# Cross-attention stack: pieces ordered by a model of four engine queues, and other group sizes

## The chip, the cores and the metric

The kernel runs on one core of one Trainium2 chip. The metric is the device time of one execution in microseconds (us), lower is better. The profile below was taken by the hardware profiler from one execution. Its engines are PE (TensorE matmuls), PEld (TensorE weight loads), DVE (VectorE), ACT (ScalarE), POOL (GpSimd) and SP (which issues most transfers). "L1326" is line 1326 of the kernel. The granted clock is the share of TensorE's full clock that the chip let it have.

## What is computed

Four transformer blocks follow one another on x of 4 x 1024 tokens, 288 wide; a context of 64 tokens per batch element is attended to in each. There are 16 heads of 18. Blocks 0 and 3 are alike and are the ones that matter here:

```python
h = layer_norm(x, ln1_g, ln1_b, 1e-06); q8, s, sm = quant_act(h)
... # self-attention with quantised q, k, v and output products
h = layer_norm(x, ln2_g, ln2_b, 1e-05)
q8, s, sm = quant_act(h)
q = quant_linear(q8, s, sm, wq2, bq2)
k = cond @ wk2.T + bk2; v = cond @ wv2.T + bv2
a = attn(q, k, v, mask)
a8, sa, sma = quant_act(a)
x = x + quant_linear(a8, sa, sma, wo2, bo2)
h = layer_norm(x, ln3_g, ln3_b, 1e-05)
q8, s, sm = quant_act(h)
h = gelu(quant_linear(q8, s, sm, wfc1, bfc1))     # 288 -> 1152
q8, s, sm = quant_act(h)
return x + quant_linear(q8, s, sm, wfc2, bfc2)    # 1152 -> 288
```

`quant_act` finds each token's largest magnitude, divides by it and rounds to levels -127 to 127. Block 1 attends without normalisation to the context in two parts (ordinary and "prompt" keys, each with a softmax and weights of its own) and adds both outputs to x. Block 2 is a block with tensor-wide quantisation; it is not touched.

## The kernel before

x stays in SBUF as 32 tiles of 128 tokens. Everything runs in one program, in order: block 0's self-attention (`quant_self`), then a stage of block 0's context attention and feed-forward with block 1's attention woven in, then block 2 (`fq_attn`), then block 3's self-attention, then block 3's context attention and feed-forward. Block 0 and block 3 share the code in `quant_net`; the argument `vip` tells them apart (it holds block 1's weights, and is given with block 0 only).

The stages in question are made of generators, one per group of tokens. A generator issues some instructions and yields; each stretch between two yields is a piece. `run_stages` holds the active generators and chooses which one goes on next, so the choice sets the order in which pieces are written down. It keeps one clock, `now`. A piece says how much PE time it takes, which moves `now` on, and how long after that its next piece may follow, a constant wait such as 6.0. A third value names the ACT table that the next piece needs: `EXP` or `GELU`. A piece of the other table than the last is put off until nothing else is ready or until it has waited 6 us. Among the ready ones the earlier stage in the list goes first. A layer underneath then places the instructions of each engine, by the order of writing and by what is ready, and inserts the waits.

The generators are:

- `ctx_stage`, context attention, 8 groups of 512 tokens (two to a batch element). A group takes its statistics (`norm_stats_of`, DVE), is normalised (`norm_apply`: ACT at L1377, then POOL times gain and plus bias, L1380 and L1381), rounded by `levels` (DVE maximum L1302, scale L1304, reciprocal L1306, then per tile DVE L1310 and ACT L1311; PE transposes L1326, ACT copy L1331), and its token scales are spread over columns (`scale_cols` DVE L2283, PE L2293, ACT L2298). A loop over four head groups follows, skewed by one step per operation: query product L2152, DVE L2160, scores L2168, ACT exponential L2171, values L2179, ACT copy L2187, transposes L2195, DVE L2198 to L2208. The result goes through `levels` again, and `level_residual` multiplies (L277), scales (DVE L1722) and adds to x (POOL L1723). The keys and values of a batch element are fetched by its first group (L2121, L2122) at the very start of that group.
- `ff_stage`, feed-forward, 16 groups of 256 tokens: statistics per 512 tokens, normalisation, output bias added to x (`add_bias`, POOL L1727), `levels` with six extra columns (`three_parts`, POOL L1587 and L1589), first product L277 with scaling and maximum on DVE (L2246), GELU on ACT (L2264, and L2266 for the maximum), `levels` again, second product, and the residual. In block 3 the tokens are then stored.
- `vip_aside`, once, in block 0: forms block 1's keys and values on PE (L2472, L2509) and stores them.
- `vip_tokens`, block 1, 16 groups of 256 tokens: transposes L2379 and L2384, query product L2399 and L2403, copies L2535, scores L2556, exponential L2564, sums L2575, reciprocal L2583, spread L2588, scaling L2597, output L2606, and the sum into x L2616.

In block 0 one context group, two feed-forward groups and two block-1 groups are active at once; in block 3 two context groups and three feed-forward groups. A feed-forward group may begin when its context group is done, a block-1 group when its feed-forward group is done. In block 0 the context and feed-forward pieces use four PSUM banks and block 1's another four; block 3 uses all eight.

Of the kernel before, what the change touches and what calls it, by code (L numbers as in the profile page):

```python
# [28 lines left out]
F32 = mybir.dt.float32  # L29
# [13 lines left out]
NG = 4  # L43
# [8 lines left out]
EXP, GELU = "exp", "gelu"  # L52
# [1126 lines left out]
class Fast(Net):  # L1179
# [60 lines left out]
    def run_stages(self, stages):  # L1240
# [5 lines left out]

        state = [{"next": 0, "busy": 0, "done": set()} for _ in stages]
        active, mode, now = [], None, 0.0

        def begin():  # L1250
            for st, sg in zip(state, stages):
                while (
# [5 lines left out]
                    active.append({"st": st, "sg": sg, "n": n, "at": now, "kind": None})  # L1258
# [5 lines left out]
        while active:  # L1264
            ready = [a for a in active if a["at"] <= now]
            if not ready:
                now = min(a["at"] for a in active)
                continue
            late = [a for a in ready if a["kind"] not in (None, mode)]
            same = [a for a in ready if a["kind"] in (None, mode)]  # L1270
            if late and (not same or now - min(a["at"] for a in late) > 6.0):
                a = min(late, key=lambda a: a["at"])
                mode = a["kind"]
            else:
                a = same[0]
# [3 lines left out]
            said = next(a["sg"][0][a["n"]], None)  # L1279
            self.pb, self.wk = outer  # L1280
            if said is None:
# [3 lines left out]
            else:  # L1285
                now += said[0]
                a["at"] = now + said[1]
                a["kind"] = said[2] if len(said) > 2 else None
# [3 lines left out]
    def levels(self, h, am, width, tag, terms=0, bufs=2):  # L1292
# [6 lines left out]
        kc = (n + terms) // width  # L1299
        if am is None:  # L1300
# [13 lines left out]
        yield 0, 6.0 if kc == n // P else 5.0  # L1314
# [3 lines left out]
        per, most = (2, kc) if kc == NC3 else (1, 5)  # L1318
        for j0 in range(0, m, per):
# [17 lines left out]
            yield 0.07 * per * kc, 1.5 if j0 + per == m else 0  # L1337
# [669 lines left out]
    def quant_net(self, L, w, ctxT, mask, out, ready=None, vip=None):  # L2007
# [4 lines left out]
        with ExitStack() as es:  # L2012
# [30 lines left out]
            for k, v in (("sw", cw["swo"]), ("b", w["bo2"])):  # L2043
                cw["wo"][k] = fp.tile([P, C], F32, name=f"wo2{k}")
                nc.sync.dma_start(cw["wo"][k], v.partition_broadcast(P))
            nb = 1 if vip else 2
            cp = pool(f"{L}cb", nb)
# [6 lines left out]
            rext = fp.tile([P, 2, 2 * B * NG], F32, name="rext")  # L2054
# [3 lines left out]
            ff_gens = self.ff_stage(g3, b3, w1, w2, tops, out, nb + 1)  # L2058
            stages = [
                (ctx_gens, nb, lambda i, d: True, None),  # L2060
                (ff_gens, nb + 1, lambda i, d: i // 2 in d[0], None),
            ]
            if vip:
# [13 lines left out]
                parts = self.key_parts(vp)  # L2077
                prep, vk = ExitStack(), []
                pk = prep.enter_context(tc.tile_pool(name="vn", bufs=1))

                def vip_pools():
                    if not vk:
# [11 lines left out]
                        lambda i, d: i in d[1] and 0 in d[2],  # L2094
# [7 lines left out]
            for n, (t, what) in enumerate(  # L2102
                ((rext, "wt"),) + (((ext, "vwx"),) if vip else ())
            ):
# [5 lines left out]
    def ctx_stage(self, cw, g2, b2, pool, nb):  # L2110
# [5 lines left out]
        keys = {}  # L2116
# [8 lines left out]
        def tokens(b, hf):  # L2125
            t0 = b * NTB + hf * 4
            if hf == 0:
                fetch(b)
            kbd, vbd = keys[b]
            stats = self.norm_stats_of(t0, 4, 1e-5)  # L2130
            yield 0, 7.0
            h = self.wk.tile([P, 4, C], F32, tag="h", name="h", bufs=nb)
            for j in range(4):
                self.norm_apply(h[:, j, :], t0 + j, stats, g2, b2, t0)
                if j % 2:
                    yield 0, 1.0 if j == 1 else 9.0
            hT, sc = yield from self.levels(h, None, CK, "x", 0, nb)
            srep = self.wk.tile([P, 512], F32, tag="srep", name="srep", bufs=nb)
            for j in (0, 2):
                two = sc[:, j : j + 2]  # L2140
                cols = self.scale_cols(two)
                yield 0, 1.0
                self.over_tokens(two, srep[:, j * P : (j + 2) * P], cols)
            yield 0.8, 1.0
            a = self.wk.tile([P, 4, C], F32, tag="h", name="a", bufs=nb)
            qs, es_, os_ = {}, {}, {}
            for n in range(NG + 3):
                g = n
                if g < NG:
# [11 lines left out]
                    yield 0.65, 0 if n else 1.0, EXP if n else None  # L2161
                g = n - 1
                if 0 <= g < NG:
# [10 lines left out]
                    yield 0.9, 0 if n > 1 else 1.0  # L2174
                g = n - 2
                if 0 <= g < NG:
# [11 lines left out]
                    yield 0.9, 0.5  # L2188
# [1174 lines left out]
```

## Time and profile before

| | us |
|---|---|
| median of 3 runs | 5224.39 (5214.77 to 5228.77) |
| the profiled execution, its own time | 5225.67 |
| its span, first to last instruction | 5224.0 |
| PE busy in the span | 4411.4 (84%) |
| ACT busy | 3066.3 (59%) |
| DVE busy | 2965.4 (57%) |
| POOL busy | 1316.5 (25%) |
| block 0's context and feed-forward with block 1 | 895 to 1707 |
| block 3's context and feed-forward | 4737 to the end |

Busy means that an instruction of that engine was running. Matmuls are pipelined, so a busy PE is not PE at its peak. Over the whole kernel PE is the busiest engine, but that share is an average over stages; the two stages that the change touches have other shares, which are read by windows. A wait in the list of waits is idle time of one engine just before an instruction, put down to what came last of that which it waited for. The mean granted clock of the whole span is 0.833.

### The profile page before, as it was taken

To read this page: it belongs to the slowest core of one execution; us is meant where nothing else is said; L and a number is where in the kernel's file an instruction comes from. 1 tells how busy PE (TensorE), PEld (TensorE's weight loads), DVE (VectorE), ACT (ScalarE), POOL (GpSimd) and SP (SyncE) were. 2 spreads that over 40 slices of the span, in tenths; PEclk is the share of its full clock that TensorE was granted. 3 is DMA by queue.
4 is the path that set the end of the run, shared out by engine and by line. 5 is a ranking of instruction groups with operands and counts; after the bars stand their busy time and mean duration, and the time that the engine had idled before them with its cause. 6 is when DMAs were issued, how large, how long until landed. Compare 5 with 4: busy or idle time off the path is not lost. (4 is left out here: it accounts for less than half of the span.)

```text
span 5224.0 us, 63236 instructions
## 1 busy us (share of the span) xinstructions
PE 4411.4 (84%) x23067; PEld 1784.7 (34%) x23067; DVE 2965.4 (57%) x6518; ACT 3066.3 (59%) x4313; POOL 1316.5 (25%) x1949
## 2 busy tenths in 40 slices
PE   5999997788888879999688873899998999996676
PEld 2223222455555431100133331454542223222334
DVE  7333244555555559999788777432334333344776
ACT  2767665455454239999788863212215766664676
POOL 4010111232322457400122225111104021003553
PEclk9999998889899975555688785899997999997778
DMA  2000002200000221000000022000000000001000
GB/s 74 4 5 12 3 21 61 80 3 14 16 12 23 90 91 38 21 0 0 21 24 25 21 96 79 24 14 10 1 10 6 8 4 9 18 21 39 12 12 20
DMA packets 135538, 135.62 MB, mean 26 GB/s; under 512 B 69260, under 2 KB 111884, under 8 KB 133552
## 3 DMA queue, kind: packets, MB, share of 16 engines
q1 hardware_dynamic: 134016, 127.79, 8.1%
q0 software_dynamic: 1200, 3.69, 0.3%
q8 instruction: 183, 3.00, 0.2%
q14 instruction: 139, 1.14, 0.1%
HBM read 79.59 MB, written 43.47 MB: 24 GB/s over the span
## 5 line engine op out<-in xcount | busy, mean ns | idle before, releaser
L1980 ACT ACTIVATE e<-ps 128x1024 f32<-128x1024 f32 x1024 | 998.9, 1021 | 484.3 <-PE ps L1970 473.5
L1970 PE MATMUL ps<-qT,kT 32*128 32x512 f32 x4096 | 705.3, 661 | 8.2 <-ACT e L1980 8.2
L1930 PE MATMUL ps<-e,v 128*32 128x512 f32 x4096 | 571.1, 623 | 10.4 <-DVE oT L1941 9.1
L2853 DVE TENSOR_REDUCE top<-e 128x2 f32<-128x2048 f32 x256 | 561.9, 2275 | 18.6 <-ACT e L2846 18.6
L2846 ACT ACTIVATE e<-ps 128x1024 f32<-128x1024 f32 x512 | 534.1, 1369 | 19.6 <-PE ps L3199 11.3
L3248 ACT ACTIVATE e<-ps 128x1024 f32<-128x1024 f32 x512 | 484.4, 1056 | 92.2 <-PE ps L3239 74.6
L3199 PE MATMUL ps<-qk 32*128 32x512 bf16 x1024 | 510.9, 604 | 24.5 <-ACT e L2846 23.2
L1723 POOL TENSOR_TENSOR x<-x,y 128x288 f32<-128x288 f32 x192 | 151.0, 798 | 980.7 <-DVE y L1722 966.1
L1380 POOL TENSOR_TENSOR h<-h,g 128x288 f32<-128x288 f32 x224 | 181.0, 810 | 721.8 <-ACT h L1377 702.6
L3251 DVE TENSOR_SCALAR eb<-e 128x2048 bf16<-128x2048 f32 x256 | 322.1, 1261 | 50.0 <-ACT e L3248 47.8
L1970 PEld LDWEIGHTS ps<-qT,kT 32*128 32x128 f32 x4096 | 205.5, 189 | 230.3 <-issue 143.1
L2846 ACT ACTIVATION_READ_ACCUMULATOR e<-ps 128x1 f32 x512 | 280.9, 550 | 0.0
L3239 PE MATMUL ps<-qk,kz 64*128 64x512 bf16 x1024 | 231.1, 449 | 41.8 <-ACT e L3248 39.2
L2399 PE MATMUL psf<-hT,w 128*128 128x512 f32 x576 | 257.9, 600 | 0.6 <-ACT hT L2391 0.6
L1377 ACT ACTIVATE h<-x,nmr,rstd 128x288 f32<-128x288 f32 x224 | 129.4, 622 | 185.8 <-DVE nmr L1369 102.5
L1326 PE MATMUL ps<-idb,q 128*128 128x128 bf16 (+2 forms) x1152 | 108.5, 245 | 151.0 <-ACT q L1311 106.8
L1930 PEld LDWEIGHTS ps<-e,v 128*32 128x32 f32 x4096 | 83.0, 109 | 421.3 <-issue 348.0
L3199 PEld LDWEIGHTS <-qk 32*128 32x128 bf16 x1024 | 52.8, 99 | 465.1 <-issue 465.1
L3148 ACT ACTIVATE gl<-psf,bf 128x512 f32<-128x512 f32 x72 | 46.0, 684 | 270.4 <-PE psf L2403 265.8
L277 PEld LDWEIGHTS <-qT 98*128 98x128 bf16 (+2 forms) x1344 | 138.7, 107 | 134.8 <-issue 51.5
L1381 POOL TENSOR_TENSOR h<-h,b 128x288 f32<-128x288 f32 x224 | 178.7, 800 | 0.3
L3152 DVE SCALAR_TENSOR_TENSOR u<-psf,bf,gl 128x512 f32<-128x512 f32 x72 | 51.2, 747 | 213.3 <-ACT gl L3148 213.0
(480 smaller groups left out, 7706.9 us busy)
## 6 DMA issues: line engine op xcount, KB each, us to landing
raw<-y SPq DMA_DIRECT2D x32, 432.0 KB
in<-raw SPq DMA_DIRECT2D x32, 432.0 KB
kz<-qk SPq DMA_DIRECT2D x128, 64.0 KB
wn<-in_L_wfc SPq DMA_DIRECT2D x12, 432.0 KB
x<-in_x SPq DMA_DIRECT2D x4, 1152.0 KB
vvo<-vt SPq DMA_DIRECT2D x16, 288.0 KB
vo<-vvo SPq DMA_DIRECT2D x4, 1152.0 KB
rawq<-y SPq DMA_DIRECT2D x32, 144.0 KB
```

The lines of the kernel that those rows point to most:

```text
L1380: nc.gpsimd.tensor_tensor(h, h, g, ALU.mult)
L1381: nc.gpsimd.tensor_tensor(h, h, beta, ALU.add)
L1930: nc.tensor.matmul(acc[i * HP : (i + 1) * HP, :], lhsT=st["v"][:, kt, h * (D + 1) : h * (D + 1) + HP], rhs=es_[i // 2][:, i % 2, :], start ...
L1970: nc.tensor.matmul(pss[i // 2][:, i % 2, :], lhsT=self.row_tile(kT, i)[:, kt * P : (kt + 1) * P], rhs=self.row_tile(qT, i)[:, qh * 512 : ( ...
L1980: nc.scalar.activation(e, ps, AF.Exp, scale=SCALE)
L2399: nc.tensor.matmul(o, lhsT=lhs(i)[:, c, :], rhs=rhs(i)[:, c, :], start=(c == 0), stop=False)
L2846: nc.scalar.activation(e[:, j, :].rearrange("p (a n) -> p a n", a=2), sc, AF.Exp, scale=rstep, accum_out=sums[:, t, h0 + j : h0 + j + 1],)
L2853: nc.vector.tensor_reduce(top[:, t, h0 : h0 + 2], e, AX.X, ALU.max)
L3199: self.nc.tensor.matmul(ps[:, c, :], lhsT=self.row_tile(qT, i)[:, g, qt * P : (qt + 1) * P], rhs=self.row_tile(kT, i)[:, g, c * 512 : (c + ...
L3239: nc.tensor.matmul(pss[i][:, n, :], lhsT=kz[rows, i, kt * P : (kt + 1) * P], rhs=qT[rows, g, qh * 512 : (qh + 1) * 512], start=True, stop= ...
L3248: nc.scalar.activation(e[:, 2 * n : 2 * n + 2, :], ps, AF.Exp, scale=step)
L3251: nc.vector.tensor_scalar(eb, e, MAGIC, MAGIC, ALU.add, ALU.subtract)
```

## The change

`run_stages` gets another model. Instead of one clock and constant waits it keeps the time at which each of four engine queues (p, d, a, g for PE, DVE, ACT and POOL) is free. A piece names its work as a short text: `"p.9&a1.4"` is 0.9 on PE, with 1.4 on ACT beginning shortly after; a space means that the next item follows when the one before has ended; `x` is time on none of them. `work` adds these up and gives the end of the piece. A piece says when its generator may go on: at that end (`None`), at once (`0`), or at the end of an earlier piece. A change of table adds 1.3 to ACT's queue. Pieces of the kind `SIDE` (work that takes no part in the table's choice) and `GELU` come before others.

The figures are constants in the code, and none of them changes what is computed. The rest of the change, by part:

- Feed-forward groups have 128 tokens instead of 256 (`m = 1`), so 32 per block. Three are active in block 0 (before: two of 256), six in block 3 (before: three of 256).
- Two context groups are active in block 0 (before: one), three in block 3 (before: two), but only one at a time may be in the loop over head groups (`loop["taken"]`). The keys and values are fetched when a group enters the loop, into one buffer in both blocks (block 3 had two).
- Feed-forward stands ahead of context attention in the list of stages.
- Statistics of a context batch element are taken once for its 1024 tokens. Range checks of the softmax sums are two reductions per context group instead of eight. The scale columns of the context groups are made on POOL instead of DVE. The feed-forward output bias is added after the first product instead of beside the normalisation.
- In block 1's preparation the next head group's weights are loaded a step ahead, into two buffers.

```diff
+        free = dict.fromkeys("pdag", 0.0)
+
+        def work(at, figures):
+            for step in figures.split():
+                start = at
+                for n, item in enumerate(step.split("&")):
+                    e, us = item[0], float(item[1:])
+                    start = max(start + min(0.5, us / 4) * (n > 0), free.get(e, 0.0))
+                    at = max(at + 0.2, start + us + 0.1)
+                    if e in free:
+                        free[e] = start + us
+            return at
...
-            late = [a for a in ready if a["kind"] not in (None, mode)]
-            same = [a for a in ready if a["kind"] in (None, mode)]
+            late = [a for a in ready if a["kind"] not in (None, SIDE, mode)]
+            same = [a for a in ready if a not in late]
             if late and (not same or now - min(a["at"] for a in late) > 6.0):
                 a = min(late, key=lambda a: a["at"])
                 mode = a["kind"]
+                free["a"] = max(free["a"], now) + 1.3
             else:
-                a = same[0]
+                a = min(same, key=lambda a: (a["kind"] not in (SIDE, GELU), stages.index(a["sg"])))
...
-                now += said[0]
-                a["at"] = now + said[1]
-                a["kind"] = said[2] if len(said) > 2 else None
+                a["end"] = work(a["at"], figures)
+                a["at"] = a["end"] if need is None else need
+                a["kind"] = kind[0] if kind else None
...
-        per, most = (2, kc) if kc == NC3 else (1, 5)
+        per, most = (min(m, 2), kc) if kc == NC3 else (1, 5)
...
-            nb = 1 if vip else 2
-            cp = pool(f"{L}cb", nb)
+            nb, m, nf = (2, 1, 3) if vip else (3, 1, 6)
+            cp = pool(f"{L}cb")
...
-            ff_gens = self.ff_stage(g3, b3, w1, w2, tops, out, nb + 1)
+            ff_gens = self.ff_stage(g3, b3, w1, w2, tops, out, m, nf)
             stages = [
+                (ff_gens, nf, lambda i, d: i * m // 4 in d[1], None),
                 (ctx_gens, nb, lambda i, d: True, None),
-                (ff_gens, nb + 1, lambda i, d: i // 2 in d[0], None),
             ]
...
-                        lambda i, d: i in d[1] and 0 in d[2],
+                        lambda i, d: {2 * i, 2 * i + 1} <= d[0] and 0 in d[2],
...
             if hf == 0:
-                fetch(b)
-            kbd, vbd = keys[b]
-            stats = self.norm_stats_of(t0, 4, 1e-5)
-            yield 0, 7.0
+                stats[b] = self.norm_stats(b, 1e-5)
+                there[b] = yield "d8.5", None, SIDE
+            while b not in there:
+                yield "x1", None, SIDE
...
-                cols = self.scale_cols(two)
-                yield 0, 1.0
+                cols = self.scale_cols(two, nc.gpsimd)
+                yield "g.9", None
...
+            while loop["taken"]:
+                yield "x1", None, SIDE
+            loop["taken"] = True
+            if b not in keys:
+                fetch(b)
+                yield "x2.5", None
+            kbd, vbd = keys[b]
...
-                    nc.vector.tensor_reduce(cw["ext"][:, 0, m : m + 1], rf, AX.X, ALU.max)
-                    nc.vector.tensor_reduce(cw["ext"][:, 1, m : m + 1], rf, AX.X, ALU.min)
                     self.add_bias(t0 + g, wo["b"])
-                    yield 0.8, 0.5 if n + 1 < NG + 3 else 1.5
+                    yield ("p.85 d1.2", None, SIDE) if g + 1 == NG else ("p.85 d1.2", 0)
+            loop["taken"] = False
+            m = 2 * b + hf
+            rf = rc.rearrange("p g t i o -> p (g t i o)")
+            nc.vector.tensor_reduce(cw["ext"][:, 0, m : m + 1], rf, AX.X, ALU.max)
+            nc.vector.tensor_reduce(cw["ext"][:, 1, m : m + 1], rf, AX.X, ALU.min)
...
-            for j in range(2):
+            for j in range(m):
                 self.norm_apply(h[:, j, :], t0 + j, stats[s0], g3, b3, s0)
-                self.add_bias(t0 + j, w2["b"])
-            yield 0, 6.0
+            yield f"a{0.6 * m}&g{1.6 * m}", None, SIDE
...
-                if j == 0:
-                    yield 1.5, 0
+                self.add_bias(t0 + j, w2["b"])
+                if j + 1 < m:
+                    yield "p1.5&d2.0", 0
...
-            yield 1.5, 2.5, GELU
-            for j in range(2):
+            yield "p1.5&d2.3&g.8", None, GELU
+            for j in range(m):
                 nc.scalar.activation(ff[:, j, :], ff[:, j, :], AF.Gelu, scale=sc[:, j : j + 1])
...
+        ahead = loads(0)
+        yield "x5", None
+        for g in range(NG):
+            wk, wv, wos = ahead
+            if g + 1 < NG:
+                ahead = loads(g + 1)
```

Every other yield of these generators is rewritten in the new form, such as `yield 0.9, 2.3` into `yield "p.9 d1.8", None`.

## The prediction

> **What bounds the kernel now.** The change touches two stretches: the context and feed-forward stage of block 0, with block 1's prompt attention woven in (895 to 1707 us), and the same stage of block 3 without block 1 (4737 us to the end). I found them from the first and last matmuls of lines 2152, 2606 and 277, read their busy times in the view by windows (columns: window, length, busy us and count of PE, weight loads, DVE, ACT and POOL, granted clock, DMA share, GB/s), then the waits inside each.
>
> ```profile
> 895.00:1707.00 812.00, 674.27 (x4013) 433.18 (x4014) 437.53 (x1339) 394.43 (x674) 238.59 (x375) 0.88 0.10 29
> 4737.00:5224.00 487.00, 315.25 (x1844) 177.19 (x1842) 318.42 (x1052) 307.96 (x483) 225.17 (x349) 0.78 0.06 21
> ...
> 900.00:905.00 5.00, 0.00 (x0) 0.00 (x0) 0.00 (x0) 0.00 (x0) 2.35 (x4) 0.50 1.00 304
> 1214.00:1216.00 2.00, 2.00 (x17) 0.55 (x14) 0.36 (x1) 1.43 (x3) 0.05 (x1) 1.00 0.76 184
> ...
> 5030.00:5080.00 50.00, 34.85 (x180) 18.53 (x181) 36.22 (x127) 38.71 (x62) 30.77 (x47) 0.73 0.02 7
> ```
>
> In block 0 PE is the busiest engine, yet idles 812 - 674 = 138 us. In block 3 no engine passes 66%: PE idles 172 us, and PE, DVE and ACT wait for one another. The last lines show the second price of a gap: the clock stands at 0.50 where PE idles and at 1.00 in dense work. If it only takes those two values, 0.88 over block 0 means half speed for 0.24 x 812 = 195 us, and 0.78 in block 3 for 0.44 x 487 = 214 us.
>
> Who holds PE up: first block 0, then block 3 (engine, line, releaser, us in total, times, longest).
>
> ```profile
> PE ps L1326 <- ACT q L1311: 53.5, 8, 19.2
> PE ps L2575 <- ACT ev L2564: 22.2, 5, 6.0
> PE ps L2556 <- ACT ev L2564: 12.1, 3, 4.8
> ```
>
> ```profile
> PE ps L1326 <- ACT q L1311: 53.2, 17, 14.5
> PE ps L1326 <- issue: 28.0, 1, 28.0
> PE ps L277 <- ACT qT L1331: 21.6, 10, 9.1
> PE ps L2293 <- DVE scol L2283: 13.1, 5, 4.4
> PE ps L277 <- DVE rext L2208: 11.0, 1, 11.0
> ```
>
> These are waits inside one group's chain, normalisation or GELU, rounding (L1311), transposes (L1326), copy (L1331), product (L277), at places where PE had no other group's work queued. In the timeline PE is empty for over 2 us 18 times in block 0 (102 us together) and 20 times in block 3 (131 us). The 28.0 us gap is block 3's start, where nothing else exists yet.
>
> **The change, part by part.** *Order and width.* Arithmetic and PE instructions stay. What changes is how much foreign PE work stands in PE's queue between the last matmul a chain starts from and the first that waits for its end. I counted this cover in the built order of both kernels, each matmul at its group's mean busy time before (median, before to after). Product to next transposes (277 to 1326): block 0 12.7 to 13.9 us, and the least from 1.9 to 5.3; block 3 17.3 to 13.5, but the least from 0.0 to 6.1. Transposes to product (1326 to 277, hiding a 0.7 us copy): 1.2 to 3.3, and 1.5 to 3.5. Same to the query product (1326 to 2152): 4.0 to 20.9, and 2.2 to 22.8. Prompt attention: query copy to scores (2403 to 2556) 1.9 to 8.7, exponentials to sums (2556 to 2575) 0.8 to 1.9. Narrower is the output turn in the context loop (2179 to 2195): 3.7 to 3.0, and 3.6 to 1.9; it hides one 0.59 us copy. The rounding chain that needs cover is about 6 us for 128 tokens: 0.55 (L2246) + 1.26 (L2264) + 0.2 + 0.2 + 0.82 (L1310) + 1.25 (L1311) + 1.28 for a table load, and small rows. Least covers of 0.0 and 1.9 fell short of it; 5.3 and 6.1 about reach it.
>
> In block 0 I take the one-group hole after the first context group (973 to 1010 us: 7.0 + 14.6 + 2.4) as filled but for 8, the first 17.7 as staying, and of the remaining 60 us of long gaps half gone: idle 138 to 92. With about half the gaps, half-clock time goes from 195 to some 110; at 80% PE work there, 85 x 0.5 x 0.8 = 34 us. Together -80. Bounds: nothing, or all long gaps but the first gone (-84) and half-clock time down to 60 (-54).
>
> *Table loads.* The built order has 47 in block 0 instead of 16 and 29 in block 3 instead of 15: 45 more.
>
> ```profile
> L2264 ACT ACT_TABLE_LOAD x9 | 11.5, 1283 | 0.2
> L2171 ACT ACT_TABLE_LOAD x7 | 9.0, 1283 | 0.1
> ...
> L2264 ACT ACT_TABLE_LOAD x8 | 10.3, 1283 | 0.1
> ```
>
> Each costs 1.283 us plus some 30 ns of gaps, 1.31: 41 us in block 0, 18 in block 3. Of the 16 in block 0, ten are followed by an idle stretch of 1.6 us or more of ACT and so cost nothing. ACT is 49% busy there; a quarter of 41 us on PE's path is +10 (bounds 0 and 41). Block 3's go into the ACT sum below.
>
> [...]
>
> *Halved feed-forward groups.* Per block 16 more of each per-group row. ACT: 16 GELUs of the maximum (0.198, L2266) and 16 more, smaller copies (0.15 each, estimated from 0.37 for 256 and 0.59 for 512 elements): +5.6. DVE: six small rows of 0.16 (+15) and a maximum of about 0.45 twice for 0.75 once (+2). POOL: 80 more rows of the three parts at 0.19 (+15). *Taken off DVE per block:* 48 of the 64 range reductions (48 x 0.158 = 7.6), 32 scale columns (0.29 each, 9) and three of the statistics chains (about 7). DVE ends at -7, within nothing. *Scale columns to POOL:* not in the trace; between a 0.19 cast and a 0.79 sum of 288 elements; I take 128/288 of 0.79, 0.35, +11 a block (6 to 25). POOL is 29% and 46% busy, which hides it. If that cover goes, this shows:
>
> ```profile
> 5015.07 6.17 DVE L1310 TENSOR_SCALAR h<-h,rsy 128x288 f32<-128x288 f32 x1
> ...
> 5021.74 2.56 PE L277 MATMUL ps<-wfc2T,qT 128*128 128x288 bf16 x10 [11.02 <-DVE rext L2208]
> ```
>
> A rounding step of 0.37 us lasted 6.17 while POOL ran eight sums without a pause, and PE idled 11.0. Another, 3.96 us, lies at block 3's start. Smaller groups shorten POOL's runs, but three context groups at the start lengthen one; I count both at zero (bounds -10 and +12).
>
> *One key buffer in block 3, fetched at the loop.* SP issues the same transfers. The fetch of the next batch's keys now waits for the last scores on the old ones; 5.4, 17.9 and 13.3 us of PE work lie between that release and first use. A fetch moved its bytes in 3 us (4905 to 4908, 132 GB/s). Hidden; without the cover 3 x 3 us, and the scores and what PE queues behind them would wait. Block 0 had one buffer already and keeps 35 us and more. *Bias sums behind the first product* and *weights one step ahead* in the prompt's keys take waits off PE (7.0 us at L2509, in the hole above).
>
> *Block 3 in sum.* ACT goes from 308 to 308 + 18 + 6 = 332 us. Outside the first 43 us it was busy 298 of 444, 67%; its best 50 us slice above had 38.7, 77%. 322 us at 80% take 402: -42. Bounds: 67% still, with covers in vain (+35), and 85% (379, -65).
>
> The profiled execution took 5225.67 us, its span 5224.0, 1.3 above the median of the runs, so no correction. 5225.7 - 80 + 10 - 42 = 5114.
>
> **The rivals.** *Only block 0 gains* (0.19): block 3's engines are evenly loaded, and ACT gets busier. For: its 24 us more of ACT; against: 131 us of long gaps while ACT idled a third of the time. 5225.7 - 70 = 5156. *The switches decide* (0.11, the other side): each extra load stands in ACT's queue ahead of something PE waits for, and the covers save nothing: 45 x 1.31 = 59, 5285. It turns the sign once cover saves under 59 us. For: PE's longest waits are on ACT; against: ACT at 49% in block 0, and over half of its loads now hidden. *The order isn't what matters* (0.04): the layer that places instructions reorders pieces anyway, and the gaps only move: 5226. Against: the covers were counted after its placing. *The clock pays more* (0.13): gaps become rare enough that half-speed stretches vanish: -138 and -65 give 5023.
>
> **How the numbers follow.** The forecast has 0.53. Faster: 0.53 + 0.19 + 0.13 = 0.85; within 0.3% (16 us, about what the spread of the three runs, 14 us, can tell from no change) 0.04; slower 0.11. The range runs from the low rival, 5025, to 5205, beyond which lie the last two rivals and a little of the second; the forecast's own is 5060 to 5155.
>
> **What would show it.** In the changed profile: PE idle in block 0 near 90 us and its clock near 0.93; the wait of the transposes on rounding (L1326 in the kernel before) well under 53 us in both; table loads 47 and 29 at 1.28 us; ACT near 80% in block 3 past its start; no wait of scores on a key fetch. The prediction is wrong if PE idle stays near 138 and 172 us, with ACT's loads named as releasers, or if DVE's rounding steps last several us in many places.

## The result and the profile after

The changed kernel takes 5177.22 us (median of 5 runs, 5169.0 to 5188.75), the kernel before 5224.39 (5214.77 to 5229.1). The ratio is 0.991 with a 95% interval of 0.989 to 0.993: 47 us or 0.9% faster, where 110 us were forecast (5114). The profiled execution took 5169.41 us, its span 5167.7.

The two stages were cut at the same landmarks in both traces: from the last matmul of a self-attention's output product to the last matmul on block 1's values (block 0) or to the end (block 3). View by windows (window, length, busy us and count of PE, weight loads, DVE, ACT, POOL, then clock, DMA share, GB/s), the kernel before first, then the changed one:

```profile
893.50:1698.80 805.30, 668.50 (x4001) 429.98 (x4000) 433.89 (x1332) 390.50 (x668) 232.08 (x365) 0.88 0.10 30
4750.10:5224.00 473.90, 306.33 (x1792) 171.58 (x1792) 308.86 (x1022) 304.78 (x479) 220.46 (x343) 0.78 0.06 20
```

```profile
889.60:1665.10 775.50, 655.24 (x4002) 414.85 (x4002) 441.84 (x1329) 431.40 (x726) 266.10 (x474) 0.89 0.10 30
4704.70:5167.70 463.00, 323.93 (x1793) 173.91 (x1792) 296.10 (x1007) 326.02 (x525) 259.37 (x455) 0.79 0.07 21
```

Block 0 became 30 us shorter and block 3 11 us. The stretch between them, which the change does not touch, took 3040 us instead of 3051; the variants below have 3043 to 3046 there with the old order and 3023 to 3043 with the new one, and why is open. PE's idle time in block 0 is 775.5 - 655.2 = 120 us (137 before, 92 forecast), and by the forecast's estimate (0.89 means half speed for 0.22 of the time where the clock takes 0.50 and 1.00 alone; the clock record of either trace has no other value) its half-clock time is 171 us (193 before at the same cut, 110 forecast). Of the 80 us that the forecast took off block 0, 46 were idle time and 34 shorter PE work; the profiles show 17 and 13. POOL has 34 and 39 us more to do, ACT 41 and 21.

What PE waits for in the changed kernel, block 0 and then block 3 (engine, tile and line, what it waited for, us in total, times, longest):

```profile
PE ps L1349 <- ACT q L1333: 18.5, 5, 15.8
PE ps L277 <- ACT qT L1354: 14.4, 5, 5.8
PE ps L2331 <- POOL scol L2319: 7.9, 3, 4.9
PE ps L2633 <- DVE xT L2628: 7.3, 4, 4.1
```

```profile
PE ps L1349 <- ACT q L1333: 49.3, 23, 15.7
PE ps L1349 <- POOL h L1405: 19.6, 1, 19.6
PE ps L277 <- ACT qT L1354: 9.6, 10, 2.7
```

The transposes' wait for rounding fell from 53.5 to 18.5 us in block 0, all but 2.7 of it the first hole of 15.8. But many new short waits stand in its place, for the copy after the transposes, the scale columns, block 1's reciprocal. In block 3 it hardly moved, 53.2 to 49.3, spread over 23 waits instead of 17.

The profile of before could have told much of why. Two steps up the chain, the rounding of ACT waits for DVE, and DVE for POOL. Here the waits name the tile: h is a normalised input, ff comes from GELU, a from the context loop. The kernel before, block 0, then block 3:

```profile
ACT q L1311 <- DVE h L1310: 101.5, 16, 14.8
DVE amx L1302 <- POOL h L1381: 80.8, 8, 14.6
DVE amy L1302 <- POOL h L1381: 25.5, 10, 3.7
ACT q L1311 <- DVE ff L1310: 11.9, 12, 1.3
```

```profile
ACT q L1311 <- DVE h L1310: 53.6, 17, 21.6
DVE amx L1302 <- POOL h L1381: 30.9, 5, 17.8
DVE amy L1302 <- POOL h L1381: 27.3, 10, 5.1
ACT q L1311 <- DVE ff L1310: 13.4, 9, 4.6
```

The changed kernel, block 0, then block 3:

```profile
ACT q L1333 <- DVE h L1332: 51.9, 22, 14.9
DVE amy L1324 <- POOL h L1405: 38.7, 22, 5.5
DVE amx L1324 <- POOL h L1405: 30.6, 7, 12.9
ACT q L1333 <- DVE ff L1332: 15.2, 12, 4.0
```

```profile
ACT q L1333 <- DVE h L1332: 44.5, 25, 11.0
DVE amx L1324 <- POOL h L1405: 37.5, 7, 15.1
DVE amy L1324 <- POOL h L1405: 22.5, 12, 3.4
ACT q L1333 <- DVE ff L1332: 4.6, 6, 1.5
```

ACT's rounding waits for normalised tiles far more than for GELU's, and those come from POOL's gain and bias (lines 1404 and 1405, 1380 and 1381 before). These are ACT's waits. PE's own waits for rounding, each followed to the tile that was rounded, say the same in block 0: 51.6 of the 53.5 us before were for h (33.8 of them in two holes at the start) and none for ff, 17.8 of 18.5 after. In block 3 they do not: of the 53.2 us before, 15.9 were for h, 19.3 for a and 18.0 for ff; of the 49.3 after, 20.6, 21.4 and 7.3. One such place in the changed kernel's timeline of block 0 (start, duration, engine, line, form; in brackets the idle time before it and what ended it):

```profile
1296.04 0.80 POOL L1404 TENSOR_TENSOR h<-h,g 128x288 f32<-128x288 f32 x1 [10.81 <-ACT h L1401]
...
1299.57 0.80 POOL L1751 TENSOR_TENSOR x<-x,wo2b 128x288 f32<-128x288 f32 x1
1300.32 0.80 POOL L1405 TENSOR_TENSOR h<-h,b 128x288 f32<-128x288 f32 x1
...
1301.07 1.55 POOL L1404 TENSOR_TENSOR h<-h,g 128x288 f32<-128x288 f32 x2
1302.57 1.54 POOL L1405 TENSOR_TENSOR h<-h,b 128x288 f32<-128x288 f32 x2
...
1304.14 1.35 DVE L1324 TENSOR_REDUCE amx<-h 128x4 f32<-128x1152 f32 x1 [4.10 <-POOL h L1405]
1305.41 0.64 DVE L1332 TENSOR_SCALAR a<-a,rsx 128x288 f32<-128x288 f32 x2
...
1305.81 0.96 ACT L1333 ACTIVATE q<-a,nmagic 128x288 bf16<-128x288 f32 x2 [4.62 <-DVE a L1332]
...
1306.79 1.28 ACT L2609 ACT_TABLE_LOAD   x1
...
1308.08 1.08 ACT L2609 ACTIVATE ev<-ps 128x512 f32<-128x512 f32 x2
...
1308.73 1.71 PE L2633 MATMUL ps<-xT,kps 32*128 32x256 f32 x5 [7.06 <-ACT ev L2609]
```

From 1296.04 POOL runs without a pause. Before that it was idle for 10.81 us, until ACT (L1401) handed it a normalised tile: here POOL starts late as well as taking long, and why ACT was late was not followed. DVE's maximum amx waits 4.10 us for it at the head of DVE's queue, so the rounding of another group's a, which is ready, stands behind it; ACT waits 4.62 us for that, and block 1's exponential, also ready, stands behind ACT's and behind a table load of 1.28 us. PE pays 7.06 us for a wait that the list puts down to an exponential.

### The profile page after: what moved, and what is told of

The parts are those of the page before. It is cut to its first block, busy times and chain, and to the rows that moved or that the text cites. A ratio compares the mean times of both kernels' runs of the same rounds, so it can differ in the third digit from the quotient of the medians.

```text
span 5167.7 us, 63518 instructions
## 1 busy us (share of the span) xinstructions
PE 4402.1 (85%) x23067; PEld 1767.0 (34%) x23067; DVE 2961.2 (57%) x6478; ACT 3131.3 (61%) x4422; POOL 1395.9 (27%) x2173
## 5 line engine op out<-in xcount | busy, mean ns | idle before, releaser
L2891 ACT ACTIVATE e<-ps 128x1024 f32<-128x1024 f32 x512 | 534.0, 1369 | 19.6 <-PE ps L3244 11.3
L3296 DVE TENSOR_SCALAR eb<-e 128x2048 bf16<-128x2048 f32 x256 | 321.9, 1261 | 49.3 <-ACT e L3293 47.0
L1401 ACT ACTIVATE h<-x,nmr,rstd 128x288 f32<-128x288 f32 x224 | 130.2, 622 | 139.2 <-DVE nmr L1393 68.1
L1354 ACT COPY qT<-ps 98x384 bf16<-98x384 bf16 (+3 forms) x256 | 151.6, 641 | 72.6 <-PE ps L1349 72.4
```

Of the source, the lines that this page charges most:

```text
L2891: nc.scalar.activation(e[:, j, :].rearrange("p (a n) -> p a n", a=2), sc, AF.Exp, scale=rstep, accum_out=sums[:, t, h0 + j : h0 + j + 1],)
L3296: nc.vector.tensor_scalar(eb, e, MAGIC, MAGIC, ALU.add, ALU.subtract)
```

## The experiments

Four theories stood against each other, for the 63 us that were forecast and did not come. *The switches*: the 45 more table loads cost more than 10 us. *Late POOL*: the normalisation on POOL delivers late. *Order and sizes*: one of the two brings a loss. And, formed later, *added POOL work*: the 73 us that the change gives POOL ate the rest.

All were timed beside the kernel before (medians of 5216 to 5221 us). "Change" is the difference of ratios times 5220 us, against the changed kernel's 0.991 for its variants and against 1 for those of the kernel before; it is uncertain by some 13 us for the former and 5 to 8 for the latter. The last columns are lengths of the two stages in the profiled executions (before 805 and 474, changed 775 and 463).

| variant of | edit | median us | ratio (95%) | change | block 0 | block 3 |
|---|---|---|---|---|---|---|
| changed | GELU left out, no table loads | 5157.85 | 0.988 (0.9863 to 0.9896) | -16 | 777 | 444 |
| before | the same | 5196.45 | 0.9964 (0.9954 to 0.9974) | -19 | 803 | 459 |
| changed | no gain and bias of the normalisation | 5024.47 | 0.9627 (0.9611 to 0.9643) | -148 | 701 | 392 |
| before | the same | 5045.33 | 0.9672 (0.9656 to 0.9688) | -171 | 715 | 389 |
| changed | sizes of before | 5303.9 | 1.0159 (1.0145 to 1.0174) | +130 | 834 | 535 |
| changed | four scale-column buffers | 5161.74 | 0.9888 (0.9873 to 0.9904) | -11 | 771 | 466 |
| changed | POOL's missing figures in the model | 5176.29 | 0.9922 (0.9907 to 0.9937) | +6 | 768 | 476 |
| changed | bias sums on DVE | 5116.17 | 0.9805 (0.979 to 0.9821) | -55 | 746 | 445 |
| before | scale columns on POOL | 5222.92 | 1.0013 (1.0004 to 1.0022) | +7 | 809 | 477 |
| changed | added POOL work on DVE | 5168.62 | 0.991 (0.9895 to 0.9925) | 0 | 781 | 461 |
| changed | residual sums on DVE | 5142.22 | 0.9859 (0.9837 to 0.9882) | -27 | 778 | 439 |
| changed | DVE's rounding step left out | 5137.24 | 0.9836 (0.9814 to 0.9858) | -39 | 767 | 437 |
| changed | statistics for four tiles | 5171.77 | 0.991 (0.9892 to 0.9929) | 0 | 764 | 471 |
| changed | no bias in the normalisation | 5076.63 | 0.9734 (0.9721 to 0.9748) | -92 | 730 | 417 |
| changed | no bias sums on x | 5104.58 | 0.9784 (0.9771 to 0.9798) | -66 | 735 | 436 |

**The switches.** The same edit in both kernels:

```diff
-                nc.scalar.activation(ff[:, j, :], ff[:, j, :], AF.Gelu, scale=sc[:, j : j + 1])
+                nc.scalar.activation(ff[:, j, :], ff[:, j, :], AF.Identity, scale=sc[:, j : j + 1])
...
-            nc.scalar.activation(am, top, AF.Gelu)
+            nc.scalar.activation(am, top, AF.Identity)
```

> The changed kernel with GELU left out: the two activations of the feed-forward stage are plain copies with a scale (Identity), so that the 47 table loads of block 0 and the 29 of block 3 are gone (76 x 1.283 us = 97 us of ACT), and every group may go on without a change of table. The order of the pieces stays as it is. Theory 'the switches' (the loads cost far more than the 10 us that were put down): this kernel falls by 60 us or more below the changed one, to 5115 us or less. Theory 'late POOL' (what is late is the normalisation on POOL, and loads only lengthen a queue that waits anyway): it falls by 15 to 40 us, to about 5150 us, and the waits of the transposes for the rounding stay.

> The kernel before with GELU left out in the same two activations (31 loads of blocks 0 and 3 gone, 40 us of ACT). Theory 'the switches': it gains little, 10 us or so, and the distance between the two kernels without GELU is 100 us or more, as forecast without the loads. Theory 'late POOL': it gains 5 to 20 us, and the distance between the two stays at 50 to 70 us.

The changed kernel loses 76 table loads and 16 us, the one before 31 loads and 19 us: the 45 loads more cost nothing that can be measured (without them the changed kernel gains 3 us less than the other, uncertain by some 14). Block 0, where 47 were taken away, stayed at 777 us against 775; block 3 gained 19 us from 29 loads and in the kernel before 15 us from 15. That the switches cost 60 us is out. The distance between the two kernels came out at 39 us, a little under the 50 to 70 expected, within the uncertainty.

**Gain and bias of the normalisation.** In both kernels, for the second and third normalisation (which then get `None`):

```diff
-        nc.gpsimd.tensor_tensor(h, h, g, ALU.mult)
-        nc.gpsimd.tensor_tensor(h, h, beta, ALU.add)
+        if g is not None:
+            nc.gpsimd.tensor_tensor(h, h, g, ALU.mult)
+            nc.gpsimd.tensor_tensor(h, h, beta, ALU.add)
```

> The changed kernel without gain and bias of the second and third normalisation in blocks 0 and 3 (gains are ones and biases zeros in these inputs, so the values stay): 128 POOL instructions of 0.80 us less in each of the two blocks, 103 us of POOL per block. The order of the pieces stays as it is. Theory 'late POOL': the waits of amx and amy for POOL (30.6 and 38.7 us in block 0, 37.5 and 22.5 us in block 3) go, PE's idle time in the two stages falls from 120 and 139 us to 90 and 110 us, and the time falls by 50 us or more, to 5125 us or less. Theory 'the switches': at most 15 us, to 5160 us or more.

> The kernel before without the same gains and biases. Theory 'late POOL' as a loss that the change brought: this one gains clearly less than the changed one does, 25 us or less, and the distance between the two opens to 70 us or more. If POOL is late in both alike, both fall by the same and the distance stays near 47 us. Theory 'the switches': at most 15 us.

Windows of the two stages, of the changed kernel without gain and bias, then of the kernel before without them:

```profile
893.00:1594.35 701.35, 640.80 (x4002) 408.95 (x4002) 426.73 (x1327) 427.47 (x725) 168.85 (x345) 0.94 0.11 33
4630.18:5022.59 392.41, 303.51 (x1792) 165.58 (x1792) 275.97 (x1007) 317.41 (x521) 159.89 (x327) 0.86 0.08 25
```

```profile
890.03:1605.20 715.17, 643.13 (x4000) 419.49 (x4000) 423.12 (x1332) 389.92 (x668) 137.40 (x237) 0.93 0.11 33
4650.92:5039.69 388.77, 290.60 (x1793) 166.57 (x1792) 280.96 (x1022) 301.88 (x479) 123.69 (x215) 0.85 0.08 24
```

206 us of POOL work less by the rows (POOL's busy time fell by 197 and 192) is worth 148 us in the changed kernel and 171 in the one before, where 25 or less had been expected if the change had brought the lateness. And POOL was never busier than 56% in a stage. So that lateness is not something that the change brought; it was there, and the change hides a little of it. With it gone, the changed kernel's block 0 idles for 61 us and runs at half clock for 84, better than the forecast's 92 and 110. And the two kernels then differ by 21 us only: with this work gone the old order too is down to 72 us of idle time in block 0, and there is less left to hide.

**Order or sizes.** The changed kernel with the group sizes of before; everything else of the change stays:

```diff
-            nb, m, nf = (2, 1, 3) if vip else (3, 1, 6)
+            nb, m, nf = (1, 2, 2) if vip else (2, 2, 3)
...
-                        lambda i, d: {2 * i, 2 * i + 1} <= d[0] and 0 in d[2],
+                        lambda i, d: i in d[0] and 0 in d[2],
```

> The changed kernel with the sizes of before: in block 0 one context group and two feed-forward groups of 256 tokens, in block 3 two and three (the condition of the third stage goes by one group instead of two). The new order, its model and the scale columns on POOL stay. Theory 'the order brings it': 5160 to 5200 us, near the changed kernel. Theory 'the sizes bring it': within 15 us of the kernel before, 5210 us or more. In the split of the forecast the sizes carry most of the cover that block 0 gains, so it expected 5190 us or more here.

Neither alone: the new order with the old sizes is 1.6% slower than the kernel before, in both stages (+29 and +61 us). PE's waits in its block 3:

```profile
PE ps L1349 <- ACT q L1333: 85.9, 33, 7.2
PE ps L1349 <- POOL q L1611: 27.9, 9, 7.1
PE ps L277 <- ACT qT L1354: 24.5, 14, 3.6
```

Rounding is waited for 85.9 us (before 53.2), POOL's three parts of the scales 27.9 (before 5.0). Followed by tile, 34.7 of the 85.9 us were for GELU's ff (7.3 in the changed kernel): in block 3 the smaller groups do shorten the waits that the forecast had counted. So the whole gain needs the sizes, which are worth 59 and 72 us in the new order. Which part of the new order loses with large groups, and what the new sizes would do in the old order, was not tried.

**Which part of POOL's work.** Three variants: the scale columns' buffers (with six instead of eight for two small statistics tiles, which makes the room), the figures that the model lacks, and the bias sums.

```diff
-            cols.append(self.tmp(P, "scol"))
+            cols.append(self.wk.tile([P, P], F32, tag="scol", name="scol", bufs=4))
```

```diff
-                    yield ("p.85 d1.2", None, SIDE) if g + 1 == NG else ("p.85 d1.2", 0)
+                    yield ("p.85 d1.2&g.8", None, SIDE) if g + 1 == NG else ("p.85 d1.2&g.8", 0)
```

```diff
-                    self.add_bias(t0 + g, wo["b"])
+                    self.add_bias(t0 + g, wo["b"], nc.vector)
...
-                self.add_bias(t0 + j, w2["b"])
+                self.add_bias(t0 + j, w2["b"], nc.vector)
```

> The changed kernel with four buffers for the scale columns instead of two (and six instead of eight for two small statistics tiles, which makes the room). With two, POOL stands at the head of its queue until PE has read the first pair: 33.0 us in 9 waits in block 0, 22.0 us in block 3, with the gains of the next normalisation behind it. Theory 'late POOL, by this wait': the waits of POOL for PE's scale product go, and the time falls by 15 us or more, to 5160 us or less. If the blocked queue costs nothing: within 8 us of the changed kernel.

> The changed kernel with the POOL work that its model leaves out put into the figures: 0.8 us for the bias sum in the last step of each context head group, and 0.8 us for that of the first token tile in groups of two. No instruction is added or taken away, only the order that the model gives may move. Theory 'late POOL, because the model counts too little of it': the order shifts the normalisation forward and the time falls by 10 to 30 us, to 5145 to 5167 us. If the model's missing POOL work doesn't matter: within 8 us of the changed kernel.

> The changed kernel with the bias sums of the context and feed-forward stages on DVE instead of POOL: 64 instructions of 0.81 to 0.85 us less on POOL in each of blocks 0 and 3 (53 us), 64 of about 0.45 us more on DVE (29 us). The order of the pieces stays. Theory 'late POOL': 10 to 30 us faster than the changed kernel, 5147 to 5167 us. Theory 'DVE is the late queue': slower than the changed kernel by 5 us or more.

The buffers cut POOL's wait for PE's scale product from 33.0 to 12.3 us in block 0; the 11 us of gain lie inside the uncertainty, inconclusive. The missing figures brought nothing, where 10 to 30 us were hoped for: the order shifts, block 0 gains 7 us and block 3 loses 13. The bias sums on DVE were worth 55 us by ratio, more than any theory had said.

**Added POOL work.** Then the change's own POOL work, 73 us, seemed the cause. Two tests: one part of it put into the kernel before, and all of it taken back in the changed kernel.

```diff
-                cols = self.scale_cols(two)
+                cols = self.scale_cols(two, nc.gpsimd)
```

```diff
-            self.three_parts(rs, [q[:, :, n + a : n + b] for a, b in ((0, 3), (3, 5), (5, 6))])
+            self.three_parts(rs, [q[:, :, n + a : n + b] for a, b in ((0, 3), (3, 5), (5, 6))], nc.vector)
...
-                cols = self.scale_cols(two, nc.gpsimd)
+                cols = self.scale_cols(two)
```

> The kernel before with one part of the change alone: its 64 scale columns of blocks 0 and 3 are made on POOL instead of DVE (some 40 us more of POOL at the 0.60 to 0.69 us that they take in the changed kernel, some 24 us less of DVE). Order and sizes of before. Theory 'POOL is the queue that sets the pace' (206 us of POOL work less was worth 172 us in this kernel): 12 to 35 us slower than before. Theory 'POOL hides it', as the forecast had it: within 8 us of before, or faster.

> The changed kernel with all POOL work that the change added put on DVE: the scale columns, and the three parts of the reciprocal scales of the feed-forward groups (32 x 5 small instructions a block, twice as many as before since the groups are half as large). That is more than the 73 us that POOL gained in the two stages (266 against 232, 259 against 220). The order of the pieces stays. Theory 'POOL sets the pace, and its added work ate the rest of the forecast gain': 30 us or more faster than the changed kernel, 5147 us or less. Rival (DVE, already 57 and 64% busy, pays as much as POOL gains): within 10 us of the changed kernel, or slower.

42 us more of POOL (255 and 240 instead of 232 and 220) cost the kernel before some 7 us (2 to 11 by the interval), and moving 102 us of POOL work (with 70 more on DVE) gave the changed kernel nothing. So as a place for this work POOL is nearly as good as DVE. Both tests moved work and took none away; what the 73 us would be worth if they were gone was not measured. That the two kernels come closer, not further apart, once POOL has 100 us less to do in each stage speaks against them as the cause.

**What makes POOL late.** Left were a queue blocked at its head by residual sums, the amount of POOL's work, the length of the chain, or any elementwise work costing as much.

```diff
-        nc.gpsimd.tensor_tensor(self.x[:, t, :], self.x[:, t, :], y, ALU.add)
+        (eng or nc.gpsimd).tensor_tensor(self.x[:, t, :], self.x[:, t, :], y, ALU.add)
```

(with `nc.vector` given by the two stages), then, in `levels`,

```diff
-            nc.vector.tensor_scalar(t, t, rs[:, j : j + 1], MAGIC, ALU.mult, ALU.add)
-            nc.scalar.activation(q[:, j, :n], t, AF.Identity, bias=self.nmagic)
+            nc.scalar.activation(q[:, j, :n], t, AF.Identity, scale=rs[:, j : j + 1])
```

and statistics per group as before (the normalisation then reads `mine`):

```diff
-            if hf == 0:
-                stats[b] = self.norm_stats(b, 1e-5)
-                there[b] = yield "d8.5", None, SIDE
-            while b not in there:
-                yield "x1", None, SIDE
+            mine = self.norm_stats_of(t0, 4, 1e-5)
+            yield "d5.5", None, SIDE
```

> The changed kernel with the residual sums (x + y) of the context and feed-forward stages on DVE instead of POOL: 64 instructions of 0.80 to 0.81 us a block less on POOL, 64 of about 0.45 us more on DVE, as many as the bias sums that were moved before (61 us faster). POOL's queue then holds nothing that waits for PE's products but the scale columns. Theory 'blocked head' (the gains of the next group stand in POOL's queue behind a residual sum that waits for a product): 60 us or more faster than the changed kernel, to 5117 us or less. Theory 'amount of POOL work': like the bias sums, 40 to 60 us faster. Theory 'DVE pays as much as POOL gains', as it was with the scale columns and three parts: within 15 us.

> The changed kernel with DVE's rounding step left out in blocks 0 and 3 (128 instructions of 0.42 to 0.91 us a block, 70 us of DVE): ACT scales by the reciprocal itself and the levels stay fractional. POOL's work stays. Theory 'any elementwise work in the chains costs as much as POOL's' (0.7 us a us): 80 to 110 us faster than the changed kernel. Theory 'POOL alone sets the pace': 30 us or less.

> The changed kernel with the statistics of the second normalisation taken for the four token tiles of each context group, as before, instead of once for a batch's eight. Theory 'the start of block 3 pays for it': the first query product comes up to 9 us earlier after the last self-attention product (35 us instead of 44), and the time falls by 5 to 15 us. Otherwise within 5 us; DVE has four more chains of some 15 small instructions in each block.

The residual sums, as many and as long as the bias sums, gave half as much (27 us against 55, and nothing in block 0), where a blocked head was to give 60 or more. That speaks against it but does not close it: the sums that wait for PE now stand in DVE's queue. DVE's rounding step, 148 us of work in the same chain, was worth 39 us, 0.26 us a us (0.35 by DVE's busy time, which fell by 110 only); POOL's gains and biases 148 of 206, 0.72. The 39 us lie between what the two theories had asked for. The statistics change nothing: the first query product of block 3 still comes 44 us after the last self-attention product.

The last pair takes equal POOL time away and gives DVE none, in the chain (the two normalisations get `None` for the bias) and beside it:

```diff
-        nc.gpsimd.tensor_tensor(h, h, beta, ALU.add)
+        if beta is not None:
+            nc.gpsimd.tensor_tensor(h, h, beta, ALU.add)
```

```diff
-                    self.add_bias(t0 + g, wo["b"])
...
-                self.add_bias(t0 + j, w2["b"])
```

> The changed kernel without the bias sums of the second and third normalisation in blocks 0 and 3 (biases are zeros, the values stay; 128 POOL instructions of 0.81 us, 103 us, which stand in the chain from statistics to transposes). Gains stay. Theory 'amount of POOL work' (0.7 us a us, from 147 of 206): 60 to 85 us faster than the changed kernel, about as much as the other run of this pair. Theory 'length of the chain': 75 us or more, and well over twice what the other run gains.

> The changed kernel without the bias sums on x in the context and feed-forward stages of blocks 0 and 3 (zeros too; 128 POOL instructions of 0.82 to 0.85 us, 106 us, which nothing waits for until the residual sum of the same token tile). Theory 'amount of POOL work': 60 to 85 us faster than the changed kernel. Theory 'length of the chain': 35 us or less, which moving them to DVE (61 us faster) already speaks against.

66 us for 106 us of sums that no rounding waits for, 92 us for 103 us in the chain: 0.62 and 0.89 us a us (0.68 and 0.94 by POOL's busy time, which fell by 97 and 98 us). Their intervals do not overlap, but the second is not "well over twice" the first, which the length of the chain alone would have asked for. So work in POOL's queue costs even where no rounding waits for it, and standing in the chain adds to it. A part of either may be DVE's: its busy time fell by 24 and 27 us too, with the same instructions. After the second of the two, DVE's maxima still wait for POOL, but less (changed kernel in block 0: 30.6 and 38.7 us):

```profile
DVE amy L1324 <- POOL h L1405: 25.6, 16, 4.8
DVE amx L1324 <- POOL h L1405: 23.3, 7, 13.2
```

**A version that beats both.** Bias sums on DVE and four scale-column buffers; then the normalisation's bias on DVE too; or, instead of that, the residual sums on DVE.

> A candidate that beats both: the changed kernel with the bias sums on DVE (5116 us alone) and four buffers for the scale columns. If the two add: 5100 to 5112 us. If the scale columns' wait is covered once POOL has less to do: 5112 to 5122 us.

> The candidate before this one, with the sum of the bias of the second and third normalisation on DVE too (another 64 instructions of 0.81 us a block from POOL, 64 of about 0.45 us to DVE, and a step that DVE's own rounding waits for). Theory 'POOL sets the pace': another 30 us or more, to 5080 us or less. If DVE becomes the late queue: not faster than the candidate before it.

> The first candidate (bias sums on DVE, four buffers for the scale columns, 5105 us) with the residual sums on DVE too. Theory 'blocked head': 5070 us or less. If DVE has no room left (55 us more a block than in the changed kernel): 5100 us or more.

They take 5104.63 us (0.9789, 0.9774 to 0.9804), 5096.85 (0.9773, 0.9758 to 0.9788) and 5093.01 (0.9757, 0.9739 to 0.9774). The first is what its two parts add up to, though the buffers' share stays within the uncertainty. The second is no clear gain on the first (30 us or more were expected of it); that DVE gives the rest back is argued from its busy time, 330 of 435 us in block 3. The third, 2.4% below the kernel before, computes everything the changed kernel does.

## Why the prediction fell short

The direction was right and the size was not: -47 us for -110.

- *The step that failed is the cover in "Order and width"*, -80 in block 0, which came out at -30. It counted PE's foreign work "from product to next transposes" against a rounding chain of about 6 us that begins at GELU. In block 0 the waits belonged to another chain, which begins at the statistics and passes POOL. Of the 61 us of long gaps (over 2 us) past the holes at the start, 18 ended with a rounded h, 34 with an exponential of block 1 and none with ff. In the kernel before without gain and bias 14 us of such gaps are left, and no exponential ends one: these waits too came from POOL's work. In the changed kernel 45 of the 61 us stayed, where 30 were forecast, and the holes at the start went from 43 to 35, where 26 were. The taking of 60 us of long gaps as half gone, and of half-clock time as 110, rested on that count. Idle time came to 120 instead of 92, half-clock time to 171 instead of 110; with gain and bias off POOL it came to 61 and 84. That POOL's work holds up PE is shown. That it is why the gain stopped at 47 us is argued: no cover was counted for POOL's chain, and without that chain's work the two kernels differ by 21 us, not by 110.
- *"POOL is 29% and 46% busy, which hides it"* was nearly right for what it was said of, the scale columns (0.64 and 0.69 us each on average, not 0.35, and 2 to 11 us of cost in the kernel before), and wrong as a reading of POOL: 0.62 to 0.89 us of the span went with each us of some of its work. What the forecast put at zero, the change in DVE steps that drag while POOL runs (the 6.17 us), was near it: no rounding step of the changed kernel's two stages takes over 1.5 us. For DVE's waits on POOL's tiles, 106 us in block 0 and 58 in block 3 before, 69 and 60 after, it had no term.
- *Table loads*, +10: the counts (47 and 29, 1283 ns) were right, and so were the 30 ns of gaps: in the trace of before a load of these two stages begins 17 to 19 ns after the instruction ahead has ended, and where its operand was ready the next activation begins 11 or 12 ns after the load. No cost was measured in block 0, though single loads stand on PE's path, as in the place above. The rival in which they decide falls.
- *Block 3 at 80% of ACT*: ACT's work was right (326 us for 332). Past the first 43 us, cut as in the forecast, ACT was busy for 316 of 433 us, 73%; that is the 31 us missing from -42. Why ACT was not kept busier is known in part only, since in block 3 PE's waits for rounding are spread over h, a and ff. One part is the start: the first query product comes 44 us after the last self-attention product instead of 35, with 19.6 us of it one wait on POOL's bias.
- *Key buffer*: no wait of scores or values on a key transfer is in the list of either stage. Right.
- The rival nearest to the time was "Only block 0 gains", 5156, though block 3 did gain a little. The forecast never parted order from sizes, and the runs show that the change without its sizes loses 83 us. That the time fell inside the stated range is due to the range's width: the sum's two main terms, -80 and -42, came out at -30 and -11.

## What to carry to other kernels

Before counting the cover for a wait, follow it back by tile through every engine's queue, and count the cover for the chain that is found there, not for the one that looks longest. An engine's busy share says little about what its work costs, as with POOL here, busy for 34% and 56% of the two stages: take a known amount of it away (inputs of ones and zeros make that free) and read the us per us, 0.62 to 0.89 here. Work moved to another engine must be paid for there, and only a run tells whether it is: the bias sums moved to DVE were worth 55 us, the scale columns and three parts nothing.

## What the runs showed of the hardware

The half clock came here without a long gap. In the changed kernel without gain and bias PE's longest gap in block 0 is 3.2 us, and still the stage has 84 us at half clock, estimated as before from its mean clock of 0.94. (The changed kernel itself comes into this stage at half clock: every window from 885 to 920 us has 0.50.) View by windows of three neighbouring stretches of 3.4 us, the middle one at half clock (the columns as above):

```profile
1202.40:1205.80 3.40, 1.37 (x11) 1.01 (x8) 0.82 (x1) 3.40 (x9) 0.00 (x0) 1.00 0.00 0
1205.80:1209.20 3.40, 3.40 (x9) 2.40 (x8) 0.00 (x0) 0.21 (x1) 0.00 (x0) 0.50 0.00 0
1209.20:1212.60 3.40, 3.40 (x17) 2.57 (x17) 0.46 (x1) 0.00 (x0) 0.00 (x0) 0.99 0.00 0
```

PE was busy for 1.37 of the first 3.4 us, with a longest gap of 2.03 us, and the next 3.4 us were granted 0.50 although PE worked all through them. In the stretch before them the clock was 1.00, in the one after them 0.99. What sets off the half clock was not shown. Half-clock time in block 0 went down with idle time, though not at one rate: from 193 and 137 us in the kernel before to 84 and 61 in this variant (1.4 us for each), but to 149 and 87 with the bias sums on DVE (0.9).

By DVE's whole busy time a bias sum took about twice as long on POOL as on DVE. With the bias sums left out, DVE was busy for 429 and 284 us in the two stages, with the sums on it for 455 and 309: 0.40 and 0.38 us for each of the 64, against 0.82 to 0.85 on POOL. By rows the distance is smaller: block 1's sums into x, of the same shape but with one operand in PSUM, have 0.45 us on DVE in the kernel before (L2616, 32 of them), POOL's bias sums of that stage 0.79 (L1727), 1.75 times as much. And beside POOL's sums DVE's own unchanged work is longer, 442 and 296 us in the changed kernel against 429 and 284 without them; the same work and sums in the order of POOL's missing figures had 433 and 293. So a sum on POOL also goes with some 0.1 to 0.2 us more of DVE, which no row of the sum itself shows, and for which no run here tells the reason.
